# One hybrid layer on one core: where a later batch's q, k, v matmuls stand, how the weight words are spread, and where convolution terms are added

## The chip, the cores and the metric

The kernel runs on one core of one Trainium2 chip. A core has a matrix engine (TensorE, PE in the profile), a vector engine (VectorE, DVE), an activation engine (ScalarE, ACT), GpSimd (POOL), and SyncE (SP), which here only issues DMAs. The metric is the device time of one execution in microseconds (us), the median of several runs. Everything is in float32.

## What is computed

The input is `x`, four batches of 512 rows by 256. Four residual layers follow one another, each on a layernorm of the running `x`: a window attention (a), a feed-forward layer, a causal attention (b), and the same feed-forward layer again.

```python
x = x + attn_a(layernorm(x))     # windows of 8 tokens in two directions
x = x + ffn(layernorm(x))        # 256 -> 2048 -> 256
x = x + attn_b(layernorm(x))     # 16 heads of 16, rope, causal
x = x + ffn(layernorm(x))        # the same weights
```

Layer a views a batch as 64 x 64 tokens of 16 channels. It makes q, k and v by a 16 x 48 matrix, splits the channels into two branches of 8, and in each branch attends within windows of eight tokens (in rows for the first branch, in columns for the second) and adds a depthwise convolution of v:

```python
qkv = tok @ qkv_w
attn = softmax(part(q) * scale @ part(k).T)
out = attn @ vw + lepe           # lepe: the convolution of v, plus its bias
att = concat([x1, x2]) @ proj_w + proj_b
tok = tok + layernorm(att) * ln_w + ln_b
```

The feed-forward layer has 4-bit weights with a scale for each block of 32. They are turned into float32 once, and used by all eight passes:

```python
vals = LUT[codes] * scales
out = (gelu_tanh(x @ Wg.T) * (x @ Wu.T)) @ Wd.T
```

## The kernel before

**Stages.** There are four windows (layer a, one for each batch), four passes f0 to f3 of the first feed-forward layer, four causal attentions, and four passes s0 to s3 of the second feed-forward layer. Window 0 runs alone at the start (the head). Then pass f0 runs with window 1 beside it, f1 with window 2, f2 with window 3; f3 and s0 to s2 run with the causal attentions beside them, and s3 alone at the end.

**How the beside is made.** `weave` writes PE's order out by hand. The feed-forward pass (`main`) is a generator that yields after each matmul of 512 columns, or each pair of 256 columns; one pass has 96 such turns. The work beside it is a generator whose yields are estimates in us. `weave` sums them, and takes one turn of `main` for each 0.86 us. In these stages only PE's order is fixed by hand; a planner places the instructions of the other engines, which are each in-order queues too. In the head the orders of PE, DVE and ACT are all as written. `queue_behind` adds an edge of issue order between two instructions of one engine.

**A pass.** `ffn` goes through two halves. In each half there are eight tiles of hidden units: two matmuls into a PSUM tile `pg`, Gelu on ACT into `gs`, two matmuls into `pu`, and the multiply `it = pu * gs` on DVE (L753). Then four output tiles `po` of eight matmuls each, each added to `X` on DVE (L770). All these PSUM tiles come from `fbank`, which has three banks, so a later matmul waits until DVE has read an earlier one.

**A window.** `window_front` normalizes the tokens of a batch (tile `xa`), transposes them into `yT` (L313 to L317), and makes q, k, v and the convolution terms with eight pairs of matmuls (`qkv` L326, `lepe` L328); ACT copies them into the tile `T`, where rows 0 to 3 are q and k, 4 and 5 are v, and 6 and 7 are the convolution terms of the two branches. `window_parts` has the steps of the attention on DVE: `products` (q times k, 2048 elements a partition, L392 and L400), `scores_here` (folds them by adds, on DVE) or `scores_piled` (adds them up on PE, by matmuls with the identity), `peak` (maximum and its subtraction), `power` (Exp on ACT), `total_here`, `shares`, `weighted` (weights times v), and `values_here` (folds on DVE and adds the convolution term) or `values_piled` (adds on PE) with `take_piled` (moves the sum and the convolution term into `att`). The head uses the piled forms for most of its parts; windows 1 to 3 (`window_middle`) use the DVE forms. `window_middle` yields twelve times. `window_back` gives `project` (transposes `att`, multiplies by the projection, squares), `turn` (an inverse root by `newton_root`, and the tile `z`), `move` (`zp`: PE moves `z` to the layout of `X`), and `add`.

**Order of a window beside a pass.** `beside_window(b)` takes the steps of `window_middle` of batch b, and after each one a step of `window_front` of batch b + 1, as long as there are any; what is left of the front comes after the middle. Then come `project`, `turn`, `move`, `add`, and the normalization for pass f of batch b.

**The words.** `dequant` turns twelve blocks of packed weights into float32: g0, u0, g1, u1, d0, d1, g2, u2, g3, u3, d2, d3, each with two DMAs and six DVE instructions, and a yield after each instruction, 72 in all. The first 21 are made in the head (12 + 2 + 1 + 4 + 2); the remaining 51 go into window 1, six after each step of its middle (`along`). Half 0 of a pass reads blocks 0 and 1 of each matrix, half 1 reads blocks 2 and 3.

**The head.** `busy(n)` issues n matmuls on the identity whose result nobody reads. Batch 0's front has three such blocks. The front of batch 1 (`ahead`) is taken in steps between the steps of window 0; its q, k, v matmuls stand in PE's order behind window 0's projection and ahead of its `zp`.

## Time and profile before

| what | value |
|---|---|
| median of 3 runs | 1039.27 us (1038.89 to 1041.39) |
| the profiled execution | 1040.86 us; span from first to last instruction 1039.2 us |
| mean granted clock of TensorE | 0.995 |
| first matmul of pass f0 / f1 / f2 / f3 | 79.34 / 197.33 / 298.33 / 393.06 us |
| PE's last matmul ends | 1035.7 us |
| a 512-column float32 matmul, two records | 0.86 us from start to start |
| a product of 2048 elements on DVE (L392) | 2.28 us |

The profile gives for each engine the time it was busy, and for each group of instructions the time its engine sat idle before it and who released it. A float32 matmul shows as two records. Matmuls are pipelined, so records of one engine overlap by a little. A stretch of the trace can be cut out, with the busy time of each engine in it and the share of full clock that TensorE was granted; "[3.70 <-DVE X L770]" behind a line says that the engine sat idle for 3.70 us before it, and that a DVE instruction of line 770, on tile `X`, released it.

### The profile page before, as it was taken

To read this page: it belongs to the slowest core of one execution; us is meant where nothing else is said; L and a number is where in the kernel's file an instruction comes from. 1 tells how busy PE (TensorE), PEld (TensorE's weight loads), DVE (VectorE), ACT (ScalarE), POOL (GpSimd) and SP (SyncE) were. 2 spreads that over 40 slices of the span, in tenths; PEclk is the share of its full clock that TensorE was granted. 3 is DMA by queue.
4 is the path that set the end of the run, shared out by engine and by line. 5 is a ranking of instruction groups with operands and counts; after the bars stand their busy time and mean duration, and the time that the engine had idled before them with its cause. 6 is when DMAs were issued, how large, how long until landed. Compare 5 with 4: busy or idle time off the path is not lost.

```text
span 1039.2 us, 13219 instructions
## 1 busy us (share of the span) xinstructions
PE 1008.2 (97%) x5042; PEld 586.6 (56%) x5042; DVE 671.7 (65%) x1581; ACT 349.6 (34%) x582; POOL 133.9 (13%) x263
## 2 busy tenths in 40 slices
PE   8989789999999999999999999999999999999998
PEld 6863545656566475564475554664644745446556
DVE  7989996848685877846586646666465576543111
ACT  2544222142212212435514435235254253451110
POOL 4100000000000012111240112310112301120000
PEclk9999989999999999999999999999999999999999
DMA  6310200000000020000000000000000000000000
GB/s 177 93 34 7 81 1 15 7 1 0 2 1 0 1 68 1 1 1 1 1 1 1 1 1 1 6 16 1 1 1 1 21 1 1 2 1 21 0 1 20
DMA packets 14254, 15.25 MB, mean 15 GB/s; under 512 B 2336, under 2 KB 10696, under 8 KB 14160
## 3 DMA queue, kind: packets, MB, share of 16 engines
q1 hardware_dynamic: 12416, 13.37, 4.3%
q10 hardware_dynamic: 1424, 0.99, 0.4%
q8 instruction: 39, 0.64, 0.3%
q0 software_dynamic: 352, 0.06, 0.1%
q14 instruction: 23, 0.19, 0.1%
HBM read 12.32 MB, written 2.10 MB: 14 GB/s over the span
## 4 chain that ended last, share of the span: by engine, by line
PE 80%; DVE 16%; issue 1%; POOL 1%; DMA 1%; ACT 1%; ACTq 0%; POOLq 0%; DVEq 0%; SPq 0%
PE pg_s L726 11%; PE pu_s L744 11%; PE po_s L761 10%; PE pg_f L726 8%; PE pu_f L744 7%; PE po_f L761 5%; PE s L912 4%; PE o L997 4%; PE sT L961 4%; PE qkv_b L851 3%; PE qkv L326 2%; DVE tq L381 2%; DVE tq L400 1%; PE qkT L888 1%; PE qkv_b L855 1%; DVE tv L467 1%
## 5 line engine op out<-in xcount | busy, mean ns | idle before, releaser
L927 DVE CUSTOM_DVE_ANT_0 junk<-s,mask 128x512 f32<-128x512 f32 (+3 forms) x256 | 110.1, 487 | 36.9 <-PE s L912 19.8
L744 PE MATMUL pu_f<-xT_f,u 128*128 128x512 f32 x256 | 126.2, 608 | 7.0 <-DVE it_f L753 6.2
L726 PE MATMUL pg_f<-xT_f,g 128*128 128x512 f32 x256 | 125.9, 606 | 6.0 <-DVE X L770 5.0
L726 PE MATMUL pg_s<-xT_s,g 128*128 128x512 f32 x256 | 126.7, 603 | 0.0
L744 PE MATMUL pu_s<-xT_s,u 128*128 128x512 f32 x256 | 125.4, 601 | 0.0
L761 PE MATMUL po_f<-d,it_f 128*128 128x256 f32 x512 | 117.9, 381 | 1.9 <-DVE X L770 1.0
L761 PE MATMUL po_s<-d,it_s 128*128 128x256 f32 x512 | 118.0, 382 | 0.0
L761 PEld LDWEIGHTS po_s<-d,it_s 128*128 128x128 f32 x512 | 95.2, 190 | 20.8 <-issue 8.8
L761 PEld LDWEIGHTS po_f<-d,it_f 128*128 128x128 f32 x512 | 95.0, 190 | 20.5 <-issue 6.1
L977 POOL TENSOR_SCALAR_AFFINE_SELECT e<-e 128x256 f32<-128x256 f32 x128 | 52.5, 423 | 344.6 <-ACT e L973 341.7
L973 ACT ACTIVATE e<-sT 128x1024 f32<-128x1024 f32 (+1 forms) x72 | 66.5, 969 | 72.0 <-PE sT L961 72.0
L744 PEld LDWEIGHTS pu_f<-xT_f,u 128*128 128x128 f32 x256 | 47.1, 193 | 61.7 <-issue 49.1
L726 PEld LDWEIGHTS pg_f<-xT_f,g 128*128 128x128 f32 x256 | 47.3, 193 | 59.2 <-issue 48.0
L726 PEld LDWEIGHTS pg_s<-xT_s,g 128*128 128x128 f32 x256 | 45.9, 190 | 56.8 <-issue 50.9
L744 PEld LDWEIGHTS pu_s<-xT_s,u 128*128 128x128 f32 x256 | 46.1, 190 | 54.4 <-issue 50.2
L735 DVE SCALAR_TENSOR_TENSOR g_s<-g_s,gs_s 128x512 f32<-128x512 f32 x48 | 33.2, 691 | 58.8 <-ACT g_s L734 58.4
L738 ACT ACTIVATE gs_f<-pg_f 128x512 f32<-128x512 f32 x48 | 28.6, 596 | 104.3 <-PE pg_f L726 84.9
L753 DVE TENSOR_TENSOR it_f<-pu_f,gs_f 128x512 f32<-128x512 f32 x48 | 32.9, 685 | 45.2 <-PE pu_f L744 45.0
L732 ACT COPY gs_s<-pg_s 128x512 f32<-128x512 f32 x48 | 28.2, 587 | 67.7 <-PE pg_s L726 67.5
L912 PE MATMUL s<-kT,qT 16*128 16x384 f32 (+3 forms) x512 | 50.0, 467 | 0.0
L770 DVE TENSOR_TENSOR X<-po_s,X 128x256 f32<-128x256 f32 x32 | 13.5, 421 | 54.0 <-PE po_s L761 54.0
L997 PE MATMUL o<-e,V 128*32 128x256 f32 (+3 forms) x512 | 44.4, 441 | 0.3 <-PE sT L961 0.3
(225 smaller groups left out, 1351.0 us busy)
## 6 DMA issues: line engine op xcount, KB each, us to landing
X<-in_x_dram SPq DMA_DIRECT2D x4, 512.0 KB
out_dram<-X SPq DMA_DIRECT2D x16, 128.0 KB
xa<-in_x_dram SPq DMA_DIRECT2D x28, 64.0 KB
pkg<-in_gate_p_dram SPq DMA_DIRECT2D x4, 256.0 KB
sbg<-in_gate_s_dram SPq DMA_DIRECT2D x4, 256.0 KB
pku<-in_up_p_dram SPq DMA_DIRECT2D x4, 256.0 KB
sbu<-in_up_s_dram SPq DMA_DIRECT2D x4, 256.0 KB
pkd<-in_down_p_dram SPq DMA_DIRECT2D x4, 256.0 KB
```

What stands on the lines that cost most here:

```text
L726: nc.tensor.matmul(pg, Wf["g"][par][q][:, o : o + P], xT[:, par, :], start=par == 0, stop=par == 1)
L735: nc.vector.scalar_tensor_tensor(g2, g2, 1.0, gs, ALU.add, ALU.mult)
L744: nc.tensor.matmul(pu, Wf["u"][par][q][:, o : o + P], xT[:, par, :], start=par == 0, stop=par == 1)
L753: behind_due(nc.vector.tensor_tensor(it, pu, gs, ALU.mult))
L761: nc.tensor.matmul(po[:, 0:W], inter[k][:, i * P : (i + 1) * P], Wf["d"][par][j // 2][:, (j % 2) * W : (j % 2 + 1) * W], start=k == 0, sto ...
L851: nc.tensor.matmul(ps[:, 0, :], xT[:, par, rows], c["wqk"][:, :, par], start=par == 0, stop=par == 1)
L912: nc.tensor.matmul(pss[hl // 2][:, hl % 2, at : at + n], qT[h0 : h0 + HD, g, i * P : (i + 1) * P], kT[h0 : h0 + HD, g, 0:n], start=True, s ...
L927: nc.vector.tensor_tensor_reduce(out=junk[:, 0:n], in0=pss[k][:, hl % 2, at : at + n], in1=c["mask"][:, 512 - n : 512], scale=1.0, scalar= ...
L961: nc.tensor.matmul(pss[hl // 2][:, hl % 2, at : at + n], kT[h0 : h0 + HD + 1, g, kt * P : (kt + 1) * P], qT[h0 : h0 + HD + 1, g, kt * P : ...
L973: nc.scalar.activation(e[:, :, 0 : 512 - at0], pss[k][:, :, at0:512], AF.Exp)
L977: nc.gpsimd.affine_select(out=diag, in_=diag, pattern=[[0, 2], [1, P]], compare_op=ALU.is_ge, fill=0.0, base=0, channel_multiplier=-1,)
L997: nc.tensor.matmul(outs[g][h0 : h0 + 32, kt * P : 512], v[:, kt, 4 * g + hl, :], e[:, hl % 2, at : at + n], start=kt == 0, stop=kt == 2,)
```

## The change

In windows 1 and 2 the front of the coming batch is run beside the middle only until `yT` is made (`until`). The q, k, v and convolution matmuls, and the copies into `T`, are emitted after `project` and `turn`, ahead of `move`, with no turn of the pass between them; after them one yield of 0.9 takes the place of the 7.2 (times 1.2 in window 1) of `turn`. The factors on the yields of the middle go from 0.76, 1.22, 1.22 to 0.9, 1.36, 1.22 for windows 1, 2, 3, and the factors 0.8 and 1.2 on `project` and `turn` of window 1 go.

Of the words, 24 are made in the head (fifteen instead of twelve in its first group), and 48 in window 1, four after each step instead of six.

The tile `sc` of the scores has two buffers instead of one. In the head, `values_piled` adds the convolution term as a ninth matmul on PE, and `take_piled` becomes a copy on ACT instead of an add on DVE. `newton_root` makes its first guess in one instruction instead of two. One block of idle matmuls goes from 16 to 12. The last output tile is added and stored in two halves of 128 columns, the second from ACT's queue.

```diff
@@ -95,8 +95,7 @@
     def newton_root(y, var, t, scale):
 
         nc.vector.tensor_scalar(var, var, scale, EPS, ALU.mult, ALU.add)
-        nc.vector.tensor_scalar(t.bitcast(I32), var.bitcast(I32), 1, None, ALU.logical_shift_right)
-        nc.vector.tensor_scalar(y.bitcast(I32), t.bitcast(I32), -1.0, float(0x5F3759DF), ALU.mult, ALU.add)
+        nc.vector.tensor_scalar(y.bitcast(I32), var.bitcast(I32), -0.5, float(0x5F3759DF), ALU.mult, ALU.add)
         for _ in range(3):
             nc.vector.tensor_tensor(t, y, y, ALU.mult)
             nc.vector.scalar_tensor_tensor(t, t, -0.5, var, ALU.mult, ALU.mult)
@@ -305,7 +304,7 @@
                     y[:, s, :], y[:, s, :], AF.Identity, bias=mean[:, s : s + 1], scale=rs[:, s : s + 1]
                 )
         if b == 0:
-            busy(16)
+            busy(12)
         yield 5.5 if b < 2 else 3.0
 
         ps = pair(f"yTp{b}")
@@ -315,6 +314,7 @@
             busy(2)
         yT = a1.tile([P, 8, P], F32, tag="yT", name=f"yT{b}")
         nc.scalar.copy(yT.rearrange("p s q -> p (s q)"), ps.rearrange("p a q -> p (a q)"))
+        state[b, "turned"] = True
         yield 1.5
 
         T = a2.tile([P, 8, 8, 8, 8], F32, tag="T", name=f"T{b}")
@@ -408,7 +408,7 @@
 
         def scores_here(br, hf):
             if hf == 0:
-                got["sc", br] = a1.tile([P, 8, 64], F32, tag="sc", name=f"sc{b}_{br}")
+                got["sc", br] = a1.tile([P, 8, 64], F32, tag="sc", bufs=2, name=f"sc{b}_{br}")
             dst = got["sc", br][:, half(hf)]
             if br == 0:
                 dst = dst.unsqueeze(2)
@@ -429,7 +429,7 @@
             mx = a1.tile([P, 64], F32, tag="mx", name=f"mx{b}_{br}")
             sx = sc
             if ("piled", br) in got:
-                sx = a1.tile([P, 8, 64], F32, tag="sc", name=f"sx{b}_{br}")
+                sx = a1.tile([P, 8, 64], F32, tag="sc", bufs=2, name=f"sx{b}_{br}")
             if br == 0:
                 sv, sxv = (t.rearrange("p s (k j) -> p s k j", k=8) for t in (sc, sx))
                 mv = mx.rearrange("p (s j) -> p s j", j=8)
@@ -493,15 +493,14 @@
         def values_piled(br, hf):
             part = tmp["v", br, hf]
             dst = bank("va", br)[:, 256 * hf : 256 * hf + 256]
-            pile(dst, [part(k, k + 1)[:, :, 0] for k in range(8)])
+            own = T[:, 6 + br, half(hf)].rearrange("p s j d -> p s (j d)")
+            pile(dst, [part(k, k + 1)[:, :, 0] for k in range(8)] + [own])
 
         def take_piled(br, hfs):
             rows = slice(4 * hfs[0], 4 * hfs[-1] + 4)
-            nc.vector.tensor_tensor(
+            nc.scalar.copy(
                 att[:, rows, :, 8 * br : 8 * br + 8],
                 bank("va", br)[:, 64 * rows.start : 64 * rows.stop].rearrange("p (s j d) -> p s j d", j=8, d=8),
-                T[:, 6 + br, rows],
-                ALU.add,
             )
 
         return dict(
@@ -767,9 +766,15 @@
                     )
                     if k % 2:
                         yield
-                behind_due(nc.vector.tensor_tensor(X[b][:, i, :], po[:, 0:W], X[b][:, i, :], ALU.add))
-                if last and half == 1:
-                    nc.sync.dma_start(out=out[b, i * P : (i + 1) * P, :], in_=X[b][:, i, :])
+
+                parts = 2 if b == B - 1 and last and half == 1 and i == 3 else 1
+                for n in range(parts):
+                    at = slice(n * W // parts, (n + 1) * W // parts)
+                    behind_due(nc.vector.tensor_tensor(X[b][:, i, at], po[:, at], X[b][:, i, at], ALU.add))
+                    if last and half == 1:
+                        (nc.scalar if n else nc.sync).dma_start(
+                            out=out[b, i * P : (i + 1) * P, at], in_=X[b][:, i, at]
+                        )
 
 
 
@@ -1106,6 +1111,14 @@
     def last_on(engine):
         return next(i for i in reversed(nc.cur_bb.bb.instructions) if i.engine == engine)
 
+    def until(work, state, b):
+
+        while (b, "turned") not in state:
+            w = next(work, None)
+            if w is None:
+                return
+            yield w
+
     def drain(work):
         for _ in work:
             pass
@@ -1169,7 +1182,7 @@
             some(front, 2)
             next(made)
             some(front, 2)
-            some(words, 12)
+            some(words, 15)
             some(front, 3)
             ahead = window_front(a1, a2, wconst, 1, window_load(a2, 1), state)
             for b in range(B):
@@ -1244,15 +1257,20 @@
             middle = window_middle(a1, a2, wconst, b, state)
             other = iter(())
             if b == 1:
-                middle = along(middle, words, 6)
+                middle = along(middle, words, 4)
             if b + 1 < B:
                 xa = window_load(a2, b + 1)
                 other = window_front(a1, a2, wconst, b + 1, xa, state)
-            yield from between(scaled(middle, 0.76 if b == 1 else 1.22), other)
+
+            yield from between(scaled(middle, (0.9, 1.36, 1.22)[b - 1]), until(other, state, b + 1))
             project, turn, move, add = window_back(a1, a2, wconst, b, state)
             for hf in range(2):
-                yield from scaled(project(hf), 0.8 if b == 1 else 1.0)
-            yield from scaled(turn(), 1.2 if b == 1 else 1.0)
+                yield from project(hf)
+            wait = sum(turn())
+            if b + 1 < B:
+                drain(other)
+                wait = 0.9
+            yield wait
             move()
             yield 0.9
             add()
```

## The prediction

> **What bounds the kernel now.** I read the page first: engine shares, then the slices.
>
> ```profile
> span 1039.2 us, 13219 instructions
> PE 1008.2 (97%) x5042; PEld 586.6 (56%) x5042; DVE 671.7 (65%) x1581; ACT 349.6 (34%) x582; POOL 133.9 (13%) x263
> PE   8989789999999999999999999999999999999998
> DVE  7989996848685877846586646666465576543111
> ```
>
> TensorE (PE) is busy for 97% of the span, and the change takes no matmul away but a few idle ones. Only 31 us without a matmul are there to be won, plus what runs at a lower clock. The busy times by stretch say where they lie.
>
> ```profile
> 0.00:78.00 78.00, 69.12 (x423) 54.44 (x424) 65.33 (x133) 33.06 (x80) 16.78 (x27) 1.00 0.36 101
> 78.00:180.00 102.00, 90.42 (x390) 49.93 (x390) 92.31 (x142) 33.27 (x75) 2.50 (x3) 0.95 0.08 25
> 180.00:280.00 100.00, 98.08 (x338) 58.54 (x340) 69.45 (x124) 25.02 (x39) 3.04 (x4) 1.00 0.01 4
> 280.00:378.00 98.00, 95.33 (x548) 58.95 (x548) 72.03 (x108) 16.82 (x25) 1.21 (x2) 1.00 0.00 1
> 378.00:1039.00 661.00, 655.22 (x3352) 364.73 (x3350) 372.55 (x1078) 241.45 (x363) 110.41 (x227) 1.00 0.02 7
> ```
>
> (Columns: stretch, length, busy PE, weight load, DVE, ACT, POOL, clock, DMA.) The 661 us after 378 are untouched but for the last store. Of the rest, 11.6 us of idle PE lie in 78 to 180, the first feed-forward pass with window 1 and the words beside it. A finer cut, at the moment when window 1's `att` is done (156.2) and at the start of pass f1 (197.3), shows two regimes.
>
> ```profile
> 78.00:156.20 78.20, 66.62 (x194) 36.00 (x194) 77.46 (x113) 26.26 (x64) 2.50 (x3) 0.93 0.09 30
> 156.20:197.30 41.10, 40.17 (x273) 27.31 (x272) 31.11 (x69) 8.02 (x12) 1.20 (x2) 1.00 0.05 14
> ```
>
> Up to 156.2 VectorE (DVE) works 77.46 of 78.2 us: it is the bound, and PE loses 11.6 us idle and runs at clock 0.93. After it PE is the bound, with 40.17 of 41.1. The waits of PE after 75 name what it stood for, and the order of time shows the seam:
>
> ```profile
> PE pu_f L744 <- DVE it_f L753: 6.2, 3, 2.7
> PE pg_f L726 <- DVE X L770: 5.0, 2, 3.7
> 135.04 3.78 PE L726 MATMUL pg_f<-xT_f,g 128*128 128x512 f32 x4 [3.70 <-DVE X L770]
> 155.87 0.41 DVE L489 TENSOR_TENSOR att<-tv,T 128x256 f32<-128x256 f32 x1
> 158.24 0.92 PE L326 MATMUL qkv<-bw,yT 128*128 128x448 f32 x2
> 160.07 0.60 PE L557 MATMUL aTp<-ident,att 128*128 128x128 f32 x4
> ```
>
> PE waits for PSUM banks which DVE frees late, because they queue behind words and window work. Then `att` is ready at 156.2, but the projection's first transpose comes at 160.07: PE's fixed order has the q, k, v matmuls of batch 2 ahead of it.
>
> [...]after the 3.70 us gap the four records take 3.78 us instead of 1.88. [...]here 2048 elements take 2.28 us[...]. [...]the trace has 0.59 (L341).
>
> **The change, part by part.**
>
> *Idle matmuls 16 to 12, twelve words to fifteen (head).* Eight records of 0.209 us (6.69/32) go, 1.67 us. The idle block ends at 13.4 instead of 15.0; batch 0's `xa` is ready at 13.14, so the transposes and T come 1.6 us earlier. But three more word steps (0.42 + 0.69 + 0.69 = 1.8 us) now stand on DVE before the first products, ending at 20.35 + 1.8 = 22.15; in before the first products began at 22.12, waiting for T. So the products don't move. What moves: the first pile starts at 24.4 instead of 25.5, its bank and `tmp` come free sooner, and the second pile ends near 32.0 instead of 32.6. Gain 0.55 us. Two queues matter: the DMAs of these words are moved on SP past batch 1's eight loads (7.94 us) and the four X loads (3.77 us), to about 7.3; they have 13 us to land, and batch 1's loads, 1.3 us later, are first read at 26.8. If the DMA were late DVE would stand still, up to 1.5 us.
>
> *Convolution terms on PE.* Three piles get a ninth part, 7.45/16 = 0.46 us each. Two fit into the 0.93 us PE idles before the third; the third adds 0.43. Two DVE adds (0.68 + 0.42) go; two ACT copies (about 0.59 and 0.40) come, in ACT's 4.46 us gap before `yT`. Behind the second copy, which waits for the third pile, stands the `yT` copy; but its transposes come after the same pile in PE's order, so it loses nothing. DVE's `values_here` comes 1.35 us earlier, but PE then does q, k, v of batch 1 back to back (58.8 to 67.3) and only then `zp`: that cover holds, what is late next is PE itself. Head: -0.55 + 0.43 = -0.1 us (-1.2 to +1).
>
> *Newton's first step.* One DVE operation of 0.2 us plus its gap, four times. In window 0 it lies beside the same 8.5 us of PE; in windows 1 and 2 beside the q, k, v now put there; in window 3 it may take 0.2 us off a 0.62 us wait. I count 0.1.
>
> *Words and q, k, v in pass f0.* DVE until `att`: the words fall from 51 to 48 steps, -1.8 us. PE's order now has 73 turns of f0 before the projection: the yields of `window_middle` sum to 46.2 us, the 48 words to 23.2, times 0.9 is 62.5, over 0.86 is 73 (before: (46.2 + 24.7) x 0.76 = 53.8, 63 turns). So more of f0's own multiplies fall before `att`: 11 then, 13 or 14 now, +1.5 us at 0.6 each. `att` is done at about 156.2 - 0.1 - 0.3 = 155.8.
> PE's work before the projection stays the same in sum: ten turns more (8.6 us) against eight pairs of q, k, v matmuls at 1.075 (8.6 us). But the load is even. In before words came six a yield for nine yields, PE idled, and the q, k, v fell into the last four yields, so PE arrived 3.9 us late. Now four words go to each of twelve yields; PE needs 65 of 78 us, 84% throughout, and should arrive within 1 us.
> After `att` PE has 23 turns (19.7), projection (2.9), q, k, v (8.6), `zp` (3.7), transposes (1.1): 36.0; before's total less 65 gives 37.6; I take 36.8. DVE's chain from the projection to z is 16 us, and PE has 17.6 us before `zp`, the new q, k, v included: no wait, with 2 us to spare. Behind `zp` wait nothing but f0's last 15 turns. T(2) is copied by ACT in that time, four at 0.91 and one at 0.59, within PE's 8.6; behind these copies on ACT stands only f0's next Gelu, which PE doesn't need at once. T(2)'s products start only after z.
> Start of f1: 155.8 + 1 + 36.8 = 193.6 against 197.3: -3.7 us (-7 to +6; a second gap like the one at 135 costs 2.7).
>
> *Pass f1.* 1.36 instead of 1.22 gives 73 turns for 65.6 plus q, k, v: the same PE work. PE's 0.63 us wait for z goes since the cover grows from 7.2 to 9.5 us: -0.3 with Newton. Pass f2 is unchanged.
>
> *Second `sc` tile.* Removes DVE's wait for Exp, 0.5 us in all (`sc` L383 from ACT `ek`), where DVE's order was filled with words: nothing, 0 to -0.5.
>
> *Last store halved.* The last PE ends at 1035.7, X add 0.42, then about 3 us of DMA. Half the add goes out 0.15 us sooner, the other half on ACT's queue 0.07 later with half the bytes: -0.1 (-0.3 to +0.2).
>
> Sum: -0.1 - 3.7 - 0.3 - 0.1 = -4.2 us. The profiled execution took 1040.86 with a span of 1039.2; the median of three is 1039.27, and I take the difference from the median: 1035.1.
>
> **Rivals.** A (0.52): as above, 1033 to 1037.
> B (0.27), PE is late again: DVE frees banks in its own order, and PE comes to the projection 4 us behind `att` as now. For it: every PE wait above is such a bank. Against: the new load is even. It leaves -0.8: 1038.5.
> C (0.10), more comes: `att` 2 us earlier, lag gone, 1 us more in the head: near 1031. Against: DVE is full.
> D (0.11), slower: DVE's in-order queue meets multiplies whose matmuls are not yet done, now that 13 stand before `att`; DVE idles, `att` comes late, and PE waits in order at the projection with nothing let past. It decides from 160 on (160 + 1 + 36.8 = 197.8). At 161.5, with 2.7 us of half clock, f1 starts at 202, +4.7, less 0.5 elsewhere: 1043.5. Against: DVE idled under 0.8 us there so far.
>
> **How the numbers follow.** 0.3% is 3.1 us, about what a measurement tells from no change. Faster: A less its upper edge (0.47) and C, 0.57. Same: B and that edge, 0.32. Slower: D, 0.11. The range 1031 to 1039 leaves out D, half of C and a little of B.
>
> **What would show it.** Right: idle PE in f0 falls though DVE stays full to about 156; the first transpose of `att` within 1 us of it; q, k, v directly behind the projection; f1 starting near 193.6; pass f0 of 114 instead of 118 us; f1 and the head nearly unchanged. Wrong: DVE idle before `att`, a clock of 0.5 at the projection, `zp` waiting for z, or a first product stalled by a word's DMA.

## The result, and the profile after

The changed kernel takes 1030.59 us (median of four runs, 1030.13 to 1031.59) beside 1039.08 for the kernel before on the same chip: the medians differ by -8.5 us, and the ratio is 0.9916 with a 95% interval of 0.9898 to 0.9933. The forecast was -4.2 us with a lower edge of 1031.0, so the direction was right and the size was half of what came.

The page of the changed kernel, in the rows that were shown of before:

```profile
span 1028.4 us, 13214 instructions
PE 1004.3 (98%) x5040; PEld 584.7 (57%) x5040; DVE 671.6 (65%) x1576; ACT 350.0 (34%) x584; POOL 134.5 (13%) x263
PE   7989899999999999999999999999999999999998
DVE  8979998847776777847477555776465575543111
```

DVE has as much work as before (671.6 against 671.7 us). The span is 10.8 us shorter: PE's busy time lost 3.9 us, and its idle time the other 6.9. The work of PE is the same but for four idle matmuls and three ninth parts. So most of the lost busy time was time at a lower clock: f0's granted clock was 0.96 before and is 0.98 now (cuts below), and by my estimate from the records this is 2.65 of the 3.9 us. Before, the four records at 106.40 took 3.68 us instead of 1.98, and the six at 135.04 and 138.61 took 5.70 instead of the 3.00 of the second execution below; now the four at 110.31 take 3.63 instead of 1.98 and the eight behind them 1.99 instead of 1.89.

Cut at the starts of the passes (length, then busy PE, weight load, DVE, ACT, POOL, clock, DMA), first the kernel before, then the changed one:

```profile
79.34:197.33 117.99, 106.15 (x461) 63.01 (x461) 107.26 (x180) 33.64 (x75) 3.71 (x5) 0.96 0.07 23
197.33:298.33 101.00, 100.01 (x460) 61.49 (x459) 70.32 (x111) 25.02 (x39) 3.04 (x4) 1.00 0.00 1
298.33:392.89 94.56, 91.89 (x425) 55.64 (x424) 66.91 (x118) 16.83 (x25) 2.70 (x5) 1.00 0.08 19
```

```profile
78.97:188.35 109.38, 102.93 (x460) 62.22 (x461) 105.00 (x174) 33.43 (x75) 4.03 (x5) 0.98 0.08 25
188.35:290.25 101.90, 100.21 (x459) 61.36 (x458) 72.74 (x112) 24.80 (x39) 3.04 (x4) 1.00 0.00 1
290.25:382.18 91.93, 91.50 (x425) 55.72 (x424) 66.12 (x116) 16.72 (x25) 2.71 (x5) 1.00 0.07 19
```

(In the trace f3's first matmul starts at 392.89; the 393.06 in the table of times is 0.2 us too late.) The difference of the two spans is read off directly: head 78.97 - 79.34 = -0.4; f0 -8.6; f1 +0.9; f2 -2.6; all that follows -0.1. Three of these five were not forecast so: f0 was -3.7, f1 -0.3, f2 0.

The seam at window 1's `att`, in order of time:

```profile
110.31 3.63 PE L743 MATMUL pu_f<-xT_f,u 128*128 128x512 f32 x4 [3.31 <-DVE it_f L752]
146.50 1.98 PE L743 MATMUL pu_f<-xT_f,u 128*128 128x512 f32 x4 [1.57 <-DVE it_f L752]
151.75 0.60 PE L556 MATMUL aTp<-ident,att 128*128 128x128 f32 x4
156.52 0.60 PE L556 MATMUL aTp<-ident,att 128*128 128x128 f32 x4
160.56 0.92 PE L326 MATMUL qkv<-bw,yT 128*128 128x448 f32 x2
145.42 0.42 DVE L489 TENSOR_TENSOR att<-tv,T 128x256 f32<-128x256 f32 x1
153.37 0.42 DVE L489 TENSOR_TENSOR att<-tv,T 128x256 f32<-128x256 f32 x1
```

(The changed kernel's lines are numbered a few lower: L743 is L744 of before, L752 is L753, L556 is L557, L773 is L770.) The q, k, v matmuls stand behind the projection, as meant. The first transposes come at 151.75, with no idle time in brackets, and that is 2.0 us *before* the last `att` is done at 153.79. They need half 0 of `att` alone, which is done at 145.84. Only the transposes at 156.52 need the rest. In the kernel before they came 3.8 us after it. There the two halves were done almost together, at 155.02 and 156.28:

```profile
154.60 0.42 DVE L489 TENSOR_TENSOR att<-tv,T 128x256 f32<-128x256 f32 x1
```

PE waits for DVE much less than before, and the waits of 75 to 383 us say for what:

```profile
PE pu_f L743 <- DVE it_f L752: 6.1, 4, 3.3
PE pg_f L725 <- DVE X L773: 1.0, 1, 1.0
PE xTp_f L701 <- DVE xn_f L681: 0.8, 1, 0.8
PE pg_f L725 <- DVE it_f L752: 0.7, 1, 0.7
```

The two waits for `X` that made 5.0 us are gone, and the 1.0 us is a new one at the start of f1. The 1.3 us of `zp` for `z` have shrunk to a single 0.4 (not among these lines); of the wait for `it`, 6.1 us stay.

### The profile page after: what moved, and what is told of

Read it like the earlier page. It is cut to its first block, busy times and chain, and to the rows that moved or that the text cites. A ratio compares the mean times of both kernels' runs of the same rounds, so it can differ in the third digit from the quotient of the medians.

```text
span 1028.4 us, 13214 instructions
## 1 busy us (share of the span) xinstructions
PE 1004.3 (98%) x5040; PEld 584.7 (57%) x5040; DVE 671.6 (65%) x1576; ACT 350.0 (34%) x584; POOL 134.5 (13%) x263
## 4 chain that ended last, share of the span: by engine, by line
PE 82%; DVE 15%; DMA 1%; issue 1%; POOL 1%; ACT 0%; ACTq 0%; SPq 0%; POOLq 0%; DVEq 0%
PE pg_s L725 11%; PE pu_s L743 11%; PE po_s L760 11%; PE po_f L760 8%; PE pg_f L725 8%; PE pu_f L743 8%; PE s L917 5%; PE o L1002 4%; PE sT L966 4%; PE qkv_b L856 3%; DVE tq L392 1%; PE qkT L893 1%; PE qkv_b L860 1%; DVE tq L381 1%; PE qkv L326 1%; DVE tq L400 1%
## 5 line engine op out<-in xcount | busy, mean ns | idle before, releaser
L743 PE MATMUL pu_f<-xT_f,u 128*128 128x512 f32 x256 | 124.7, 604 | 6.1 <-DVE it_f L752 6.1
L743 PE MATMUL pu_s<-xT_s,u 128*128 128x512 f32 x256 | 125.4, 601 | 0.0
L760 PE MATMUL po_s<-d,it_s 128*128 128x256 f32 x512 | 118.0, 382 | 0.0
L743 PEld LDWEIGHTS pu_f<-xT_f,u 128*128 128x128 f32 x256 | 47.3, 191 | 63.1 <-issue 51.3
L743 PEld LDWEIGHTS pu_s<-xT_s,u 128*128 128x128 f32 x256 | 46.1, 190 | 54.4 <-issue 50.2
L752 DVE TENSOR_TENSOR it_f<-pu_f,gs_f 128x512 f32<-128x512 f32 x48 | 32.6, 686 | 30.6 <-PE pu_f L743 30.6
L773 DVE TENSOR_TENSOR X<-po_s,X 128x256 f32<-128x256 f32 (+1 forms) x33 | 13.5, 413 | 53.6 <-PE po_s L760 53.6
```

The source lines that it names most:

```text
L743: nc.tensor.matmul(pu, Wf["u"][par][q][:, o : o + P], xT[:, par, :], start=par == 0, stop=par == 1)
L752: behind_due(nc.vector.tensor_tensor(it, pu, gs, ALU.mult))
L760: nc.tensor.matmul(po[:, 0:W], inter[k][:, i * P : (i + 1) * P], Wf["d"][par][j // 2][:, (j % 2) * W : (j % 2 + 1) * W], start=k == 0, sto ...
```

## The experiments

All runs of the kernel before, beside these, have medians of 1039.0 to 1040.4 us and single runs from 1036.9 to 1044.4. Ratios are to the kernel before on the same chip.

### The same kernel again

```text
the kernel before, unchanged
```

> The kernel before once more, for a second trace of it. The first profiled execution took 1040.86 us where the median was 1039.08. If that excess is an accident of the clock, passes f1 and f2 take again 101.0 and 94.6 us and only the stretch from 79 to 197 differs, 118.0 then and 116 to 118 now. If f2's idle time is an accident too, f2 comes out below 94.

One run: 1037.16 us, with a span of 1035.3, 3.9 us below the first profiled execution. Head 78.29 instead of 79.34, f0 115.2 instead of 118.0, and f1, f2 and the rest the same to 0.1 us. PE's waits in f0 stand in the same places and differ by 0.3 us at most. The difference in f0 is at the gap that the prediction showed at 135.04, with four records in 3.78 us behind it. In the second execution:

```profile
133.99 1.98 PE L726 MATMUL pg_f<-xT_f,g 128*128 128x512 f32 x4 [3.70 <-DVE X L770]
```

The same 3.70 us gap, and full speed after it. That is 1.8 us for these four records and 0.9 for the next two (1.92 us in the first execution, 1.02 here). So a single pair of traces can be off by some 3 us in f0 alone, and the -8.6 of f0 above is -5.8 against this execution. Taking the other stages from the traces (-0.4 + 0.9 - 2.6 - 0.1 = -2.2), the median difference of -8.5 leaves about -6.3 for f0.

### One part alone

Each takes its lines of the change into the kernel before. b_sc takes the second buffer (the same in `sx`), b_words the two numbers of the words, b_qkv the move of q, k, v with its factors, and b_rest the four small parts: the shorter idle block, the ninth matmul with ACT's copy, the guess in one step, and the last store in halves.

```diff
-                got["sc", br] = a1.tile([P, 8, 64], F32, tag="sc", name=f"sc{b}_{br}")
+                got["sc", br] = a1.tile([P, 8, 64], F32, tag="sc", bufs=2, name=f"sc{b}_{br}")
```

```diff
-            some(words, 12)
+            some(words, 15)
-                middle = along(middle, words, 6)
+                middle = along(middle, words, 4)
```

```diff
...
-            yield from between(scaled(middle, 0.76 if b == 1 else 1.22), other)
+            yield from between(scaled(middle, (0.9, 1.36, 1.22)[b - 1]), until(other, state, b + 1))
...
+            if b + 1 < B:
+                drain(other)
+                wait = 0.9
...
```

```diff
-            busy(16)
+            busy(12)
...
-            pile(dst, [part(k, k + 1)[:, :, 0] for k in range(8)])
+            pile(dst, [part(k, k + 1)[:, :, 0] for k in range(8)] + [own])
...
```

> The kernel before with two tiles of local scores and nothing else. Theory S, that the second tile lets 2.2 us of window work (the second branch's folds and peak) go ahead of the first Exp, off the burst that delays the X adds: -2 to -3 us, most of it in pass f2 (94.6 to about 92.5), with the wait of 1.31 us for an X add gone. As the prediction had it (only 0.5 us of waits on VectorE go): 0 to -0.5 us.

> The kernel before with the words spread (fifteen in the head's first group, four a step) and nothing else. Theory W, that bunched words made TensorE wait in pass f0: f0 falls from 118.0 by 4 or more, the q, k, v matmuls staying where they are. Theory Q, that the place of the q, k, v matmuls limits: f0 falls by 1 to 2 us only, since TensorE still reaches the projection 8.6 us of q, k, v late.

> The kernel before with q, k, v of the coming batch behind the projection, with the new factors, and nothing else; the words are still six a step. Theory Q: f0 falls from 118.0 by 4 or more. Theory W: the words still fill VectorE for nine steps of twelve, and TensorE, which now has more turns of f0 beside them, waits more for its banks: f0 falls by less than 2 us, or not at all.

> The kernel before with the four small parts alone (idle matmuls 16 to 12, the convolution terms as a ninth matmul with ACT's copy, Newton's first guess in one instruction, the last store in two halves), words and sc and the q, k, v matmuls as before. Theory joint: the small parts are worth what the sum gave them, 0.1 to 0.5 us, 1038.8 to 1039.2, ratio 0.9995. Theory share (each part has its own fixed share of the 8.5 us and the three large parts alone left most of it unexplained): the small parts hold the missing 5 to 6 us, 1033 to 1034.

| kernel | median us (runs) | ratio, 95% interval | f0 | f1 | f2 |
|---|---|---|---|---|---|
| b_sc | 1040.33 (12) | 1.0005, 0.9992 to 1.0019 | 116.9 | 101.5 | 93.8 |
| b_words | 1038.18 (20) | 0.9989, 0.998 to 0.9998 | 115.2 | 101.0 | 94.6 |
| b_qkv | 1038.88 (12) | 0.9991, 0.9973 to 1.001 | 114.1 | 102.7 | 93.3 |
| b_rest | 1038.73 (22) | 0.9993, 0.9981 to 1.0006 | 117.8 | 100.8 | 94.3 |
| all (the change) | 1030.59 (4) | 0.9916, 0.9898 to 0.9933 | 109.4 | 101.9 | 91.9 |

The four ratios together make 0.9978, or -2.3 us. The change brings -8.7 by its ratio, so some 6 us belong to no part alone. None of the large gains came that theories S, W and Q gave to one part (2 to 3 us to b_sc, 4 or more in f0 to b_words or b_qkv). The f2 of b_sc is 0.8 us shorter, with no gain in the median. Beside e_before, whose f0 took 115.2, the f0 of b_words is no shorter and that of b_qkv is 1.1 us shorter (2.8 and 3.9 beside the first execution). b_rest came out as the joint theory had it. What holds b_qkv back is in its trace:

```profile
156.81 0.63 PE L558 MATMUL aTp<-ident,att 128*128 128x128 f32 x4 [2.14 <-DVE att L490]
```

With the q, k, v matmuls out of the way PE comes to the projection in time, and then stands 2.14 us for DVE's `att`, for half 0 of it, which is done at 156.66; half 1 follows 1.27 us later. With the words spread alone half 0 is done at 145.65 and half 1 at 153.93. But q, k, v still stand ahead of the projection in PE's order, up to its very start:

```profile
155.35 0.91 PE L326 MATMUL qkv<-bw,yT 128*128 128x448 f32 x2
156.33 0.60 PE L557 MATMUL aTp<-ident,att 128*128 128x128 f32 x4
```

### One part taken out of the change

The same diffs the other way round, on the changed kernel. a_norest lacks the four small parts.

```diff
-                got["sc", br] = a1.tile([P, 8, 64], F32, tag="sc", bufs=2, name=f"sc{b}_{br}")
+                got["sc", br] = a1.tile([P, 8, 64], F32, tag="sc", name=f"sc{b}_{br}")
```

```diff
-            some(words, 15)
+            some(words, 12)
-                middle = along(middle, words, 4)
+                middle = along(middle, words, 6)
```

```diff
-            yield from between(scaled(middle, (0.9, 1.36, 1.22)[b - 1]), until(other, state, b + 1))
+            yield from between(scaled(middle, 0.76 if b == 1 else 1.22), other)
```

> The changed kernel with one tile of local scores again. Alone the second tile took 1.5 us of TensorE waits out of pass f0 (12.6 to 11.1) and 0.8 us out of f2, but no time in the median. Theory add, that waits add up and the parts are independent: +1 to +3 us over the changed kernel, half of it in f2. Theory joint, that the parts only pay together, since a wait taken away in one place is waited for at the next until all are gone: +4 us or more, nearly all in f0.

> The changed kernel with the words as before (twelve in the head's first group, six a step). Theory add: the 2.8 us of waits that spreading took out alone come back, +3 to +5 us[...]. Theory joint: +6 us or more in f0, since VectorE is full for nine steps while TensorE now has more turns of f0 beside them.

> The changed kernel with q, k, v of the coming batch back in the window's middle, and the factors of before. Theory add: +0.5 to +2 us (1.4 us of waits in f0, and 0.9 us gained in f1). Theory joint: +4 us or more in f0; TensorE comes late to the projection again, though att is done at about 152.

> The kernel before with the second score tile, the spread words and the moved q, k, v, without the four small parts (idle matmuls, convolution terms on TensorE, Newton's first step, halved last store). By the prediction these are worth 0.4 us together: -8 us against the kernel before. If they are worth more, as VectorE in f0 and the head would have to show, -6 or less.

| kernel | median us (runs) | ratio, 95% interval | f0 | f1 | f2 |
|---|---|---|---|---|---|
| a_sc1 | 1034.17 (6) | 0.9933, 0.9911 to 0.9954 | 109.7 | 102.7 | 93.1 |
| a_words | 1034.01 (6) | 0.9934, 0.9913 to 0.9955 | 111.6 | 102.3 | 91.9 |
| a_qkv | 1035.78 (12) | 0.996, 0.9946 to 0.9974 | 112.5 | 101.6 | 93.6 |
| a_norest | 1030.86 (4) | 0.9907, 0.9873 to 0.9941 | 109.4 | 102.5 | 92.2 |

By the medians each of the three large parts is worth 3.4 to 5.2 us when the other two are there (3.1 to 4.9 beside a_norest, which ran with them), and about 1 us or nothing without them. By the ratios, in which the wider spread of the kernel before counts too, it is 1.8 to 4.6. The small parts are worth 0.3, within the noise. These three runs alone do not decide between the theories: a_qkv comes nearest to the joint one (3.1 us more of f0), a_words lies in the range of the other, and a_sc1 lies between, with 0.3 us of it in f0. That the parts pay jointly rests on how little the parts bring alone, and on the waits at the projection. With the words as before, PE waits at the same place as in b_qkv:

```profile
117.73 4.15 PE L760 MATMUL po_f<-d,it_f 128*128 128x256 f32 x18 [3.54 <-DVE it_f L752]
157.93 0.63 PE L556 MATMUL aTp<-ident,att 128*128 128x128 f32 x4 [2.45 <-DVE att L489]
```

So two limits meet at the projection, PE's arrival and DVE's half 0 of `att`, and lifting one shows the other. What moves half 0 is the spread of the words. In all eight traces with six words a step the halves are done 1.27 us apart, b_qkv and a_words among them; in all ten with four a step it is 8.0 to 8.6 us, b_words among them. With six a step the words run out early (at 141.4 in the kernel before), and DVE's order then mixes the folds of the last two products; with four a step words stand between them, and half 0 goes first.

The second `sc` tile acts in f2. The kernel before, on DVE, at window 3's end, and PE's wait that follows:

```profile
327.33 0.69 DVE L753 TENSOR_TENSOR it_f<-pu_f,gs_f 128x512 f32<-128x512 f32 x1 [2.74 <-PE pu_f L744]
328.12 0.76 DVE L383 TENSOR_TENSOR sc<-tq 128x256 f32<-128x256 f32 x2
329.78 1.03 DVE L439 TENSOR_REDUCE mx<-sc 128x64 f32<-128x512 f32 x1
331.18 0.63 DVE L440 TENSOR_TENSOR sc<-sc,mx 128x512 f32<-128x512 f32 x1
...
341.88 0.74 DVE L770 TENSOR_TENSOR X<-po_f,X 128x256 f32<-128x256 f32 x2
342.34 1.98 PE L726 MATMUL pg_f<-xT_f,g 128*128 128x512 f32 x4 [1.31 <-DVE X L770]
```

In the changed kernel the second branch's last fold, maximum and subtraction stand eight microseconds after f2's start, ahead of the stretch in which DVE idles:

```profile
298.43 0.42 DVE L383 TENSOR_TENSOR sc<-tq 128x256 f32<-128x256 f32 x1
298.88 1.04 DVE L439 TENSOR_REDUCE mx<-sc 128x64 f32<-128x512 f32 x1
300.44 0.68 DVE L440 TENSOR_TENSOR sc<-sc,mx 128x512 f32<-128x512 f32 x1
332.05 0.42 DVE L773 TENSOR_TENSOR X<-po_f,X 128x256 f32<-128x256 f32 x1
```

With one tile the second branch's scores may only be written when Exp has read the first's. That Exp stands on ACT behind the last Gelu, at 327.45, so 2.4 us of DVE work (0.76 + 1.03 + 0.63) had to come in the burst after it, while DVE had idled three times 2.74 us just before. The adds into `X` came late behind it, and PE waited 1.31 us for a bank. In b_sc this wait is gone; in a_sc1 it is back with the same 1.31 us (at 335.89). In f1 one tile costs only together with the move of q, k, v: b_qkv and a_sc1 wait 0.85 us for an `X` there (at 241.03 and 239.18), and no other trace does. The move of q, k, v does the other part of f2: before has waits of 0.38 and 0.35 us at 304 and 306, b_sc and a_qkv have 0.96 us at that place, b_qkv and the changed kernel none. The guess in one step cuts the wait of `zp` in f2 from 0.62 to 0.40; a_norest, without it, has 0.64.

### The pace

The factor on the middle of window 1 is 0.76 in a_slow, as below, and 1.02 in a_quick.

```diff
-            yield from between(scaled(middle, (0.9, 1.36, 1.22)[b - 1]), until(other, state, b + 1))
+            yield from between(scaled(middle, (0.76, 1.36, 1.22)[b - 1]), until(other, state, b + 1))
```

> The changed kernel with the factor on window 1's steps back at 0.76 instead of 0.9, everything else as changed: about (46.2 + 23.2) x 0.14 / 0.86 = 11 turns of f0 fewer stand before the projection. Theory order (the pace has to fit where the q, k, v matmuls stand): TensorE runs out of turns and waits up to 9 us for att at the projection, att itself 1 us earlier since fewer multiplies stand before it, and these turns come after it: f1 starts 6 to 8 us later, 1036.5 to 1038.5. Theory load (VectorE's load until att sets the start of f1, whatever TensorE's order): f1 within 1 us of the changed kernel, 1029.5 to 1031.5.

> The changed kernel with the factor on window 1's steps at 1.02 instead of 0.9: ten turns of f0 more stand before the projection, about 83 of 96. Theory order: TensorE has 8.3 us more to do before the projection and two or three more multiplies stand on VectorE ahead of att; TensorE comes to the projection late, and the turns left behind it fall from 23 to 13, so that zp may wait for z: f1 0 to 4 us later, 1030.6 to 1034.5. Theory slack (TensorE still waits some 5 us for banks before att, and turns put there fill these waits): 1028 to 1030.

a_slow: 1040.0 us (14 runs), ratio 1.0003, 0.9989 to 1.0017. The whole gain is gone. Cut at the first transposes of `att`:

```profile
80.05:151.60 71.55, 59.91 (x166) 31.84 (x167) 71.55 (x105) 22.99 (x60) 3.32 (x3) 0.93 0.08 30
151.60:200.39 48.79, 46.80 (x296) 31.30 (x294) 42.68 (x82) 10.54 (x15) 1.21 (x2) 1.00 0.04 12
```

DVE is full to the projection all the same, which comes only 1.2 us sooner after the start of f0 than in the changed kernel (71.55 against 72.78). But PE has done 22 records less by then (the 11 turns of the expectation), and does them afterwards: 48.8 us instead of 36.6. The loss is 11 us of f0, more than the 6 to 8 expected; f1 gives 2.2 of it back. The theory of the order holds, though the wait is not where it was expected: PE does not stand at the projection but earlier, for banks (3.94, 2.49 and 3.14 us).

a_quick: 1030.9 us (6 runs), ratio 0.9911, 0.9891 to 0.9931, the same as the change and at the lower end of what the theory of order allows. PE comes to the projection 77.0 us after f0's start instead of 72.8 and leaves less behind it. In its f0 it stands 2.42 us for a bank, and then for the normalization, since no turns are left to cover it:

```profile
189.69 1.32 PE L701 MATMUL xTp_f<-ident,xn_f 128*128 128x128 f32 x8 [3.24 <-DVE xn_f L681]
```

So the factors 0.9 and 1.02 give the same time, and 0.76, which was made for the old place of q, k, v, loses the whole gain.

### More words in the head

```diff
...
             w["values_here"](1, 1)
+            some(words, 3)
...
```

> The changed kernel with three more word steps (1.8 us of VectorE work) in the head, in the 2.35 us that VectorE stands idle at 54.17 to 56.52 for the first transposes of window 0's projection; 45 steps instead of 48 are left for window 1. Theory load (VectorE's work until att sets the start of f1): att 1.8 us earlier, pass f0 1.8 us shorter, the head unchanged, near 1028.8. Theory full (TensorE's own work until the projection, 65 us plus its remaining waits, now ends later than att): att earlier but the first transposes not, pass f0 within 0.5 us of the changed kernel, 1030 to 1031. If the words' transfers are late or they delay pr, the head is 1 us longer, 1031.5.

1033.25 us (6 runs), ratio 0.9931, 0.9912 to 0.9951: 2.7 us slower than the change. Three steps fewer in window 1 did not bring `att` sooner: its last part starts at 157.84, 76.3 us after f0's start, against 74.4 in the changed kernel. Each word step also counts in `weave`'s sum, which left one turn of f0 fewer before the projection (71 instead of 72), and the planner set DVE's order anew: two more multiplies (14 instead of 12) and the first step of the projection's half 0 (`pr`) now stand ahead of the last `att`. The head itself is as long as in the changed kernel: 71.3 us from the matmul of the means to f0's start in both. So the 2.6 us by which f0 starts later in this trace are the landing of `xa`, the last part of which came at 9.29 us. Its f0 has only 5.7 us of waits but runs 1.4 us longer: half speed struck twice, at the first matmuls of the pass too, behind a gap of only 0.68 us (the changed kernel's four records there took 1.98 us):

```profile
81.58 3.48 PE L725 MATMUL pg_f<-xT_f,g 128*128 128x512 f32 x4 [0.68 <-ACT xT_f L704]
113.53 3.78 PE L743 MATMUL pu_f<-xT_f,u 128*128 128x512 f32 x4 [3.31 <-DVE it_f L752]
```

Both theories fall. At these two places PE took 3.0 us more than in the changed kernel, where only the second was slow: 3.48 + 2.12 us for the first eight records of the pass and 3.78 + 3.06 for twelve from 113.53, against 1.98 + 1.88 and 3.63 + 1.99. How much of this is in the 1.4 us is not shown; what the rest of the 2.7 us is stays open.

### The start of the head

In the traces so far f0's start lies between 77.2 and 82.2 us, for the larger part because the last part of `xa` lands at different times (the matmul of its means starts at 7.64 us in a_qkv and at 10.11 in a_words). These four runs ask whether that luck is part of the 8.5 us.

A memset of the first packed tile, behind the statistics of `xa` on DVE, holds the first words' transfer back. n_hold is the changed kernel with it, b_hold the kernel before.

```diff
             for s in range(8):
...
+            if b == 0:
+                nc.vector.memset(first_pk[:, 0:8], 0)
...
-            pk = take(I32, f"pk{n}", at < 6, 0)
+            pk = take(I32, f"pk{n}", at < 6, 0) if at else first_pk
...
+        first_pk = take(I32, "pkg0", True, 0)
```

> The changed kernel, in which the first words' transfers are issued only when VectorE has taken the statistics of all eight parts of xa (one small memset of the first packed tile on VectorE, on which the transfer has to wait). In the traces so far the last part of xa was there between 6.3 and 10.0 us, and the first matmul of f0 followed the matmul of its means (7.4 to 10.96 us) by 70 to 72 us. Theory contention (the words' transfers, issued at 3.45 us behind those of xa, delay its last parts): all of xa by 6.0, the means at 6.7, f0 starting at 78.0, the median 1 us lower, 1029.6, and the words there in time, since VectorE comes to them at 11.7. Theory start-up (the transfers of xa come at different times by themselves): the last part still between 6.3 and 10, 1030.6 or more. If the held words come late, VectorE stands for them at 11.7 and the head is as long as before or longer, 1031 to 1032.

> The kernel before with the same hold on the first words' transfers. Theory contention: 1 us lower as well, 1038.1, so that the difference of the two kernels with a fixed start of the head is still 8.5 us and none of it is the luck of xa's landing. If a part of the 8.5 us was that luck, the two differ by less than 7.5 us, 1037 or lower here with 1030 there.

n_hold took 1043.21 us (22 runs, ratio 1.0029, 1.0019 to 1.0038), b_hold 1049.4 (6 runs, 1.0081, 1.0062 to 1.01). The edit did something else than meant: the planner let batch 1's loads pass the held words on SP's queue. In n_hold:

```profile
7.66 2.52 SPq L224 DMA_DIRECT2D xa<-in_x_dram  x4
10.23 2.24 SPq L236 DMA_DIRECT2D X<-in_x_dram  x4
12.58 1.02 SPq L633 DMA_DIRECT2D pkg<-in_gate_p_dram  x1
24.89 0.43 DVE L638 TENSOR_SCALAR dwg<-pkg 128x512 int32<-128x512 int32 x1 [11.77 <-DMA pkg<-in_gate_p_dram]
```

DVE stood 11.8 us for the first words, and f0 started at 93.47. The passes after it kept their lengths to 0.7 us (110.1, 101.8, 91.9): the start of the head goes into the time one for one.

n_hold2 and b_hold2 pin SP's queue as well: the first scales behind their packed words, and batch 1's `xa` and the loads of X behind the first words.

```diff
+            if b == 1:
+                queue_behind(ins, words_last[0])
...
-        nc.sync.dma_start(out=X[b], in_=x[b].rearrange("(i p) w -> p i w", p=P))
+        ins = nc.sync.dma_start(out=X[b], in_=x[b].rearrange("(i p) w -> p i w", p=P))
+        queue_behind(ins, words_last[0])
...
```

> As n_hold, with the order of SP's queue now kept (in n_hold batch 1's eight loads of xa and the four of X had gone ahead of the held words, which came at 24.9 us): xa, then the held g0, u0, g1, then batch 1. Theory contention: VectorE's statistics run without a wait and end near 6.9 as in b_hold, the means at 7.1, the words' first transfer goes out near 7.2 and lands near 10.5, ahead of the 12.5 us at which VectorE comes to it; f0 starts near 78.2, the median 1029.5 to 1030.5 and with fewer runs above it. Theory start-up: f0 starts as before at 79 or later, 1030.6. If the held transfer lands after 12.5 us, each us of it is a us of the time: 1031 to 1033.

> As b_hold with SP's order kept: the kernel before with the head's start free of the words' transfers. Theory passes (the 8.5 us of the change lie in f0 and f2): the difference between this kernel and n_hold2 is 8 to 10 us, this one 1038 to 1039. Theory luck: under 7.5 us.

With SP's order kept: n_hold2 1030.34 us (6 runs, 1029.35 to 1031.12; ratio 0.9906, 0.9889 to 0.9924), b_hold2 1039.0 (22 runs; 0.9992, 0.9983 to 1.0). The hold gains 0.2 us of the changed kernel's median, and of the kernel before 0.4 by the median and 0.8 by the ratio, which is hardly more than noise. The two differ by 8.7 us, as the pair without it does, and as the theory of the passes had it. So the 8.5 us lie in the passes. Nor do the words' transfers alone make `xa` late: in b_hold2, where they were held, DVE still waited 0.89 us for a part of it at 7.71. What sets its landing stays open. n_hold2 also shows the 3.31 us gap of the changed kernel with full speed after it:

```profile
109.72 1.98 PE L750 MATMUL pu_f<-xT_f,u 128*128 128x512 f32 x4 [3.31 <-DVE it_f L759]
```

## Where the prediction was right and where it failed

*What bounds.* Right. DVE is full up to `att` (73.68 of the 73.75 us from 78 to the first transposes), PE without a gap after it (36.60 of 36.60). The remainder behind the first transposes was set at 36.8 and is 36.6.

*The head.* Right in its steps: the last word ends at 22.05 (22.15 in the prediction), the first pile starts at 24.31 (24.4), the second branch's maximum follows at 31.92 (32.0). Its gain is 0.4 us instead of 0.1 in this pair of traces, which is less than two executions of one kernel differ. Newton, the convolution terms and the last store came out as small as said.

*The step that failed first: "`att` is done at about 156.2 - 0.1 - 0.3 = 155.8".* It was done at 153.79. The words gave their 1.8 us. But of f0's multiplies 12 stand before `att`, not 13 or 14, which is 0.9 us; DVE's one idle spell of 0.54 us, in the sum of before, went as well; the head gave 0.3 more than counted; the last 0.3 us are not attributed. More turns before `att` did not put more multiplies on DVE in proportion, since the last two of them were put right behind it (at 153.70).

*The step that failed most: PE "should arrive within 1 us of `att`".* The prediction treated `att` as one event that PE follows. It is four writes, and the first half of the projection needs two of them. In the trace of before this made no difference, since the halves were done 1.27 us apart. But the spread of the words, a part of the change itself, put 8 us between them (b_words and a_words show it). In the changed kernel half 0 was done 5.9 us before PE came, so PE, whose own work then set the pace, went through the first transposes 2.0 us ahead of the last write. Together with the 1.0 us of lag that was allowed this is 3.0 us; with the 2.0 of the step before and 0.2 of the remainder, f1 starts 5.2 us before the forecast 193.6. Rival C named these two, "`att` 2 us earlier, lag gone", and was given 0.10 with "Against: DVE is full". That was no reason against it: a full DVE can still do the needed work first. b_qkv and a_words show the same seam with half 0 of `att` as the limit, 2.14 and 2.45 us.

*Second `sc` tile: "nothing, 0 to -0.5".* Priced as a wait of DVE, 0.5 us. It was a bar on the planner: 2.4 us of DVE's work could not be put where DVE idled. Taking it back out costs 1.2 us of f2, 0.8 of f1 and 0.3 of f0 in the traces. The medians have 3.6 us; part of the rest may be the landing of `xa` (f0 of a_sc1 started at 80.75), but that is not shown.

*"Pass f2 is unchanged".* It lost 2.6 us: 1.31 by the second tile, about 0.7 by waits near its start that go with the move of q, k, v, 0.2 by Newton; the rest is not attributed. The prediction had asked of f1's and f2's PE work only, and not what an earlier `T` lets DVE do before the pass starts.

*Pass f1: -0.3, measured +0.9.* The wait of `zp` for `z` went, 0.63 us, as said. Two new waits came, 0.99 us for `X` at 192.94 and 0.69 for `it` at 197.34. b_qkv has 1.02 us at the first of these places, but so has a_qkv, without the move, 1.24 us, while a_slow, with an f0 of 120.3, has none and an f1 of 99.7. So the move alone is not the cause. It looks as if PE, when it ends f0 early, has to wait there for what DVE has not yet done; no run tests this.

*The lower clock.* The prediction read the half speed behind the 3.70 us gap as a fixed part of the time. It does not strike each time: behind this gap the four records took 3.78 us in the first execution (granted clock 0.50 from 135.04 to 138.82), in b_hold and in b_hold2, and 1.98 in e_before. The forecast of 114 us for f0 is only 1 us below the 115.2 of e_before, while the measured 109.4 is 5.8 below it. So a good part of the forecast gain lay within the spread of the kernel before, and the larger real gain lay elsewhere.

In the changed kernel half speed behind the 3.31 us gap cost f0 nothing. It struck in the first trace (3.63 us for four records, granted clock 0.53 from 110.31 to 113.94), not in n_hold2 or a_norest (1.98), and f0 took 109.38, 109.39 and 109.39 us. Instead, PE had less to wait for DVE: waits of 0.59 and 0.36 us that n_hold2 has are not there, and the one at 146.50 is 1.57 us instead of 1.79. In the kernel before, PE came to the projection after `att`, and the same loss went into f0 (118.0 against 115.2). Runs of the kernel before lie between 1036.9 and 1044.4 us, and the fourteen of the changed kernel, a_norest and n_hold2 between 1029.4 and 1031.9. The three gaps over 2.2 us in the old f0 (2.69, 2.22, 3.70) have become one (3.31); fewer gaps and this cover would both narrow the spread, and no run separates them.

What decides is not shown. The 3.70 and 3.31 us gaps have half speed behind them in one execution and not in another. Behind the 2.69 us gap the four records take 3.68, 3.41, 3.68 and 3.67 us in before, e_before, b_hold and b_hold2, while behind 2.71 us in a_sc1 they take 1.98:

```profile
105.36 3.41 PE L744 MATMUL pu_f<-xT_f,u 128*128 128x512 f32 x4 [2.69 <-DVE it_f L753]
110.81 1.98 PE L743 MATMUL pu_f<-xT_f,u 128*128 128x512 f32 x4 [2.71 <-DVE it_f L752]
```

(The first line is from e_before.) Behind these gaps of the kernel before PE lost 1.4 to 2.7 us when half speed struck (3.41 against 1.98 for four records, up to 3.78 + 1.92 against 1.98 + 1.02). The 3.70 us gap cost PE 2.7 us in one execution and nothing in the other, so it was no fixed price. How much of a loss went into f0 depended on who came last at the projection: 2.8 us in the kernel before, nothing in the changed one.

## What to carry over

When a stage has two limits that meet at one instruction, price the change against both together: here each of the three large parts alone measured as about 1 us or nothing. Before you write "waits for X", look how many writes X is made of, which of them the waiter reads, and whether the change moves them apart. Price a missing buffer by the work that it keeps out of idle time, not by the wait that the trace shows at it. And take a second trace of the kernel before: a stretch that differs by 3 us from one execution to the next is no base for a forecast of 4.

## What the runs showed of the hardware

The same gap is followed by half speed in one execution and by full speed in another: after 3.70 us the same four records took 3.78 us in before, b_hold and b_hold2 and 1.98 in e_before; after 3.31 us they took 3.63 in the changed kernel and 3.78 in n_words, and 1.98 in n_hold2 and a_norest. The granted clock was 0.50 behind the first in before (135.04 to 138.82) and 0.53 behind the second in the changed kernel (110.31 to 113.94). The length of the gap alone did not decide it: 2.69 us had 3.41 to 3.68 us behind them in all four of before, e_before, b_hold and b_hold2; 2.71 us in a_sc1 had 1.98, and 3.54 us in a_words (the line at 117.73 above) had eighteen records in 4.15 us, as many as a_norest has in 4.15 us after 0.58. In n_words half speed also struck behind a gap of 0.68 us at the start of f0, two microseconds after one of 0.96 (3.48 us for the four records); in the kernel before, the same place has gaps of 0.96 and 0.67 us and then 1.98. The idle matmuls of the head ran at 0.209 us a record in the kernel before (32 records in 6.69 us) and at 0.170 in b_qkv (32 in 5.45).
